# Re-ordering and re-placing a Strassen transformer block: score tiles key half first, and PSUM banks as halves of two-bank tiles

## The chip, the cores and the metric

The kernel runs on one core of a Trainium2 chip. The metric is the time of one execution on the device in microseconds (us); three executions of the kernel before took 662.69, 663.8 and 662.54 us, a median of 662.69. A core has five engines that run at the same time, each its own instruction queue in order: TensorE (PE) multiplies matrices into PSUM, which has eight banks of 512 fp32 values on each of 128 partitions; VectorE (DVE), ScalarE (ACT) and GpSimd (POOL) do element-wise work, of which DVE and ACT read PSUM in this kernel and POOL works on SBUF alone; SyncE (SP) issues the DMAs. Engines wait for one another by semaphores, and an instruction that waits holds back all that stands behind it on its engine.

## What is computed

A cross-attention transformer block in fp32, for 8 sequences of 256 tokens with 512 features, and as many context tokens:

```python
x = layer_norm(hidden_states, ln1_w, ln1_b)
q = (x @ q_w + q_b)      # 16 heads of 32; k and v likewise from ctx
k = (ctx @ k_w + k_b)
v = (ctx @ v_w + v_b)
scores = einsum('bhqd,bhkd->bhqk', q, k) / sqrt(32)
attn = softmax(where(mask, scores, finfo.min))
hidden = einsum('bhqk,bhkd->bhqd', attn, v) @ cproj_w + cproj_b + hidden_states
y = layer_norm(hidden, ln2_w, ln2_b)
y = gelu_tanh(y @ fc_w + fc_b)          # 512 -> 2048
out = hidden + y @ proj_w + proj_b      # 2048 -> 512
```

## The kernel before

The 2048 tokens are done in two groups of 1024 (four sequences each), named by a digit g that is 0 or 1. Every large product goes by Strassen's scheme: a 2 x 2 block product is seven block products P1 to P7 of sums and differences of the blocks. The helper `quad` (L848) accumulates the seven in three PSUM banks X, Y, W and takes them out in steps that DVE or ACT do: `t1, c11, t2, t3, c22, c12, c21`. fc and proj use the scheme on two levels, so they have outer products 1 to 7 with inner products 1 to 7 each. The helper `sums` (L827) makes the sums of blocks; each such sum may be done by DVE (one instruction of 1024, 512 or 256 columns) or by POOL (where 1024 columns take two instructions of 512, L625 to L628).

Names in this document are built so: letters for the tile, then group and block. `c`, `x` and `y` are the transposed context, first-norm and second-norm tokens; `c0t`, `x1t`, `a0t` their block sums; `y0i1_2` the second inner sum of the first outer operand of fc in group 0; `fw` and `pw` the weights of fc and proj, `fw0i..`, `pw1i..` their sums, which go to DRAM and come back as `fl` and `pl` when wanted; `h` the hidden tiles of fc; `z` the sums of h for proj (`z1i4_4` is one); `fc011_P6`, `pd14_P4`, `q1_0_P6` and `v0_0_P1` are products of fc, proj, q and v; `turn_y0_10` is a group of PE transposes through PSUM.

Attention runs in 32 units, each four heads of one sequence. In a unit, `scores` (L1009) and `attend` (L1057) issue:

- `s`: 16 row-tiled matmuls give scores with keys on partitions, in four banks (one per head), each with two key halves of 256 queries.
- `ev`: eight ACT instructions take these out with the mask bias into two SBUF tiles `pr` of 1024 columns, two heads each.
- `mx`, `mt`, `mc`, `fold`: DVE and ACT reduce to the maximum over the keys. It is stored (`md`) and loaded back broadcast to all partitions (`mm`, four heads of 256 queries).
- `less`: subtracts the maximum, for each `pr` by one DVE instruction of 1024 (L1042) or two POOL instructions of 512 (L1047).
- `exp`: one ACT instruction of 1024 per `pr` (L1050).
- `av`: 32 column-tiled matmuls, half of them giving the row sums with a block of ones; `r` (three DVE instructions, L1073 to L1076) inverts the sums and `att` (DVE) scales.

The order of all work is written out by hand. `PROGRAM` (L124) lists 2953 operations; each engine's queue is the subsequence of its operations, and a suffix `:A`, `:V` or `:G` chooses ACT, DVE or POOL where there is a choice. `PLACES` (L355) gives every buffer its SBUF slot or PSUM bank. `Order.run` (L94) reads both, and the program is issued in that order. A buffer in a place waits for the last readers of the buffer that had the place before. SBUF slots of kind "Q" have 1024 columns, and buffers of kind "P" (512) are halves of such a slot's tile (`halves`, in `tile_of`, L556). PSUM had two kinds, three banks "W" for `quad` and five "C" for the rest, though `PLACES` may name a bank of the other kind for a buffer; each buffer is a new [128, 512] tile of its bank.

The main loops, from the end of the kernel's body: inputs and attention of group 0, q, k, v of group 1, sums of fc's weights, attention of group 1, output projection and second norm of group 0, fc of group 0, sums of proj's weights, the same for group 1, proj of group 0, fc and proj of group 1. `PROGRAM` interleaves these streams. Attention of group 1 (units 1..) thus overlaps `y0` and the first fc products.

Of the kernel before, what the change touches and what calls it, by code (L numbers as in the profile page):

```python
# [10 lines left out]
F32 = mybir.dt.float32  # L11
# [5 lines left out]
P = 128  # L17
# [6 lines left out]
BANKS = {"W": 3, "C": 5}  # L24
# [19 lines left out]
class Order:  # L44
# [49 lines left out]
    def run(self):  # L94
# [30 lines left out]
cq0_00_1 cq0_00_0 vw00 cq0_01_1 cq0_01_0 rows8 rows7 cq0_10_0 turn_c0_00 rows0 turn_c0_10 c0_00:A cq0_10_1 c0_10:V  # L125
cq0_11_0 small v0_0_P1 cq0_11_1 kw01 turn_c0_11 fw0_01_0 v0_1_P1 c0_11:A vw11 rows5 turn_c0_01 rows2 turn_c0_30
vw10 c0_01:A turn_c0_20 mk c0_30:A c0t1:G c0_20:V v0_0_t1:A vw01 turn_c0_21 v0_1_t1:V turn_c0_31 fw0_11_1 k0_0_P2
c0_21:V rows3 c0_31:V c0t2:V kw10 k0_1_P2 rows4 kw11 c0t3:V kw00 rows6 v0_0_P2 vws1:V fw0_10_0 c0t4:V fw0_00_0
v0_1_P2 vws2:V fw0_00_1 kws1:V xt0_3 rows1 k0_1_P1 fw0_10_1 kws2:V mk~1 xt0_0 kws3:V fw0_11_0 v0_0_c11 fw0i1_1:G
v0_1_P6 fw1_00_1 vws4:V xt0_2 fw0i1_2:V fw0s3:V fw1_00_0 k0_0_P1 v0_1_t2:A xt0_6 fw0i7_1:V fw1_10_0 v0_1_c11  # L130
fw0i7_2:G fw1_11_0 cols v0_1_P5 cols~1 qw10 k0_0_t1:V qw11 fw0i7_4:V fw0s1:V xt0_1 v0_0_P6 v0_1_t3:A fw1_11_1
fw0s2:V fw1_10_1 xt0_5 k0_0_P6 fw0i6_3:V xt0_4 k0_1_t1:V fw0i6_1:G cb fw0i5_1:G v0_1_P3 k0_0_t2:V kws4:G fw0i1_4:V
k0_1_P6 stats_x0_30 fw0i1_3:G fw1i1_1:V stats_x0_00 fw0i6_2:G k0_0_P5 fw1i1_3:V k0_1_t2:A xt0_7 v0_0_t2:V fw1i1_2:G
fw0_01_1 stats_x0_10 fw1i1_4:G fcd0_1_True aggr_x0_30 k0_1_P5 fw1i4_1:V qw01 aggr_x0_00 stats_x0_01 fw1i4_2:G
fw1_01_0 fw0i6_4:V fcd0_6_False stats_x0_11 k0_1_P7 k0_1_t3:A fw1_01_1 aggr_x0_01 fw0i7_3:V k0_0_t3:A eps_x0_0
fcd0_7_False stats_x0_31 pow_x0_0 qw00 aggr_x0_31 k0_1_P3 fw1i4_4:G k0_1_c22 fcd0_7_True fw0i5_2:G aggr_x0_11
fcd0_5_False nb_x0_0 k0_0_c11 fw0i5_4:G norm_x0_01:A v0_0_P5 aggr_x0_10 k0_1_c11 fw0i2_1:G norm_x0_00:A fw1i4_3:V
k0_1_c12:A fw0i2_2:V k0_0_P7 eps_x0_1 eps_x0_3 fw0i5_3:V stats_x0_20 pow_x0_3 stats_x0_21 pow_x0_1 k0_0_P3 nb_x0_3
nb_x0_1 fw0i2_3:V norm_x0_31:A aggr_x0_20 aggr_x0_21 eps_x0_2 fw0i2_4:V norm_x0_10:A pow_x0_2 k0_0_c22 fcd0_2_True
k0_1_P4 v0_0_t3:V fw1i2_1:G fcd1_4_True k0_0_c12:A fcd0_6_True norm_x0_11:A nb_x0_2 fw0s4:V kd0_0_11 k0_0_P4  # L140
fcd1_1_True vws3:V norm_x0_20:A fcd0_3_False fw1i2_2:V fcd0_5_True norm_x0_21:A qws1:V turn_x0_10 norm_x0_30:A
fw1i2_4:G k0_0_c21 turn_x0_00 x0_10:A turn_x0_20 turn_x0_30 x0_20:A v0_0_P3 x0_30:V qws3:G xt1_2 cb1_02 x0_00:V
v0_1_c12:A fw0i3_1:V turn_x0_31 fw1i2_3:V turn_x0_11 fw0i3_2:V x0_31:A turn_x0_21 fw1s1:V turn_x0_01 q0_0_P1
x0_01:A qws2:G v0_0_c12:V fcd1_5_False x0_21:A k0_1_c21 fcd1_2_True fw1i5_3:G cb1_20 x0_11:A q0_0_P2 cb1_03
q0_0_t1:A x0t1:V q0_1_P1 fw0i3_3:V q0_0_c11 x0t2:V s000 fw0i3_4:V x0t3:V q0_0_P6 ev000_11 ev000_31 fw1s3:V xt1_3
ev000_10 ev000_01 cb1_12 q0_0_P7 x0t4:V kd0_0_21 q0_0_t2:A fcd1_7_False q0_1_t1:A fw1s2:V ev000_21 ev000_00 q0_0_P5
mx000_0 fw1s4:G fcd1_6_False cb1_10 q0_1_P6 q0_0_t3:A ev000_30 q0_0_c22 ev000_20 stats_x1_10 fcd1_3_False q0_1_P2
fw1i3_3:V fw1i5_1:V q0_1_t2:V fw1i5_2:G mx000_1 q0_0_P4 fw1i6_1:G qws4:G q0_1_c11 q0_1_P5 q0_0_c21 fw1i5_4:V mt000
fw0i4_3:G fcd1_5_True mc000_3 mc000_2 s020 cb1_13 mc000_1 fw1i6_3:G fold000 cb1_00 fw1i7_1:V q0_0_P3 md000 ev020_30
fw0i4_1:V ev020_21 fw1i7_2:V cb1_23 ev020_00 fw0i4_2:G cb1_21 ev020_10 fw1i7_4:G ev020_20 cb1_01 q0_1_P7 ev020_01  # L150
cb1_11 fw1i3_1:G ev020_31 q0_0_c12:A mx020_1 fw1i6_2:G ev020_11 s002 fw1i3_2:G mm000 mx020_0 fw0i4_4:G v0_1_P7
fw1i7_3:G mt020 stats_x1_11 mc020_2 mc020_3 fw1i6_4:G q0_1_t3:V ev002_30 ev002_11 fw1i3_4:G aggr_x1_10 aggr_x1_11
v0_0_P7 mc020_1 q0_1_c22 ev002_01 ev002_00 fold020 ev002_10 eps_x1_1 md020 ev002_31 pow_x1_1 ev002_20 q0_1_P3
fcd1_7_True v0_0_c22 ev002_21 cb1_31 nb_x1_1 mx002_0 less000_1:G mm020 s022 mx002_1 cb1_33 cb1_22 v0_0_P4 ev022_20
cT1_10 cb1_32 ev022_30 cT1_00 ev022_11 cb1_30 less000_0:G ev022_31 mt002 v0_1_c22 ev022_21 q0_1_P4 ev022_00 mx022_1
mc002_2 ev022_01 ev022_10 less020_0:G mx022_0 v0_1_P4 mt022 q0_1_c21 mc022_2 mc022_3 s010 mc022_1 v0_0_c21 mc002_3
# [24 lines left out]
ev023_30 mc003_1 ev023_10 att012 ev023_11 xT1_20 s011 exp001_0 fold003 mx023_0 md003 v1_1_P2 ev011_00 mm021
ev011_31 xb1_12 ev011_11 ev011_20 xb1_11 exp001_1 v1_1_P3 xb1_03 v1_1_c11 ev011_30 mx023_1 ev011_01 ev011_21
# [329 lines left out]
def tile_xattn_block(  # L512
# [986 lines left out]
```

## Time and profile before

| | |
|---|---|
| three runs | 662.54, 662.69, 663.8 us |
| profiled execution, span from first to last instruction | 662.0 us |
| mean granted clock of TensorE | 1.000 |
| busy PE / DVE / POOL / ACT | 654.6 / 585.7 / 374.8 / 342.4 us |
| DMA | 144.84 MB, mean 219 GB/s, 206586 packets |
| median landing time of a broadcast maximum (`mm`, 512 KB) | 5.1 us |
| median landing time of a proj weight block (`pl`, 256 KB) | 4.2 us |

The profile is of one execution of its own, for which only the span is given. The difference between a run's time and the span lies ahead of the first and behind the last instruction of the trace. Engine busy times overlap, so they don't add up to the span. In group rows, "out<-in" are tile names without their numbers, then shapes, count, total busy us, mean ns of one, and idle time ahead of them with what ended it.

### The profile page before, as it was taken

What the parts mean: (1) busy time and instruction counts of PE and PEld (TensorE: products, weight loads), DVE (VectorE), ACT (ScalarE), POOL (GpSimd) and SP (SyncE); (2) the same over time, 40 slices, a digit from 0 to 9 for tenths busy, and PEclk for the clock granted to TensorE, in tenths of its full rate; (3) what the DMA queues carried; (4) which work ended last, traced back from release to release, by engine and by line L of the source; (5) the groups of instructions that cost most, each with busy time, mean ns of one, the idle gap of its engine ahead of it and who ended that gap; (6) DMA issues with size and microseconds to landing.
All of it is one profiled execution on the core that took longest, in us unless ns stands there. A gap on an engine that the chain in (4) does not pass through costs nothing.

```text
span 662.0 us, 11469 instructions
## 1 busy us (share of the span) xinstructions
PE 654.6 (99%) x3925; PEld 490.0 (74%) x3925; DVE 585.7 (88%) x980; ACT 342.4 (52%) x702; POOL 374.8 (57%) x340
## 2 busy tenths in 40 slices
PE   8999999999999999999999999999999999999997
PEld 7746554477544776777688888888888888888887
DVE  2998799999999999999999998997789787998775
ACT  2046479799999899866995572030020013930000
POOL 1262773646888997699958774423535217720260
PEclk9999999999999999999999999999999999999999
DMA  8999888786574467886878698889978779359366
GB/s 250 311 356 307 211 197 291 267 255 125 144 241 161 144 202 234 263 268 197 266 249 273 198 235 225 289 269 230 195 193 241 190 201 242 93 142 240 106 141 111
DMA packets 206586, 144.84 MB, mean 219 GB/s; under 512 B 117008, under 2 KB 166976, under 8 KB 206528
## 3 DMA queue, kind: packets, MB, share of 16 engines
q1 hardware_dynamic: 206528, 144.11, 76.8%
q8 instruction: 31, 0.51, 0.3%
q14 instruction: 27, 0.22, 0.1%
HBM read 104.10 MB, written 39.98 MB: 218 GB/s over the span
## 4 chain that ended last, share of the span: by engine, by line
PE 92%; DVE 5%; ACT 1%; DMA 1%; issue 0%; SPq 0%; POOL 0%; DVEq 0%; ACTq 0%
PE pd_X L639 15%; PE fc_X L639 14%; PE fc_W L639 8%; PE av L639 7%; PE pd_W L639 7%; PE s L639 4%; PE o_X L639 4%; PE q_X L639 4%; PE k_X L639 4%; PE v_X L639 4%; PE pd_Y L639 4%; PE fc_Y L639 4%; PE q_W L639 2%; PE k_W L639 2%; PE v_W L639 2%; PE o_W L639 2%
## 5 line engine op out<-in xcount | busy, mean ns | idle before, releaser
L1047 POOL TENSOR_TENSOR pr<-pr,mm 128x512 f32<-128x512 f32 x84 | 110.4, 1346 | 22.8 <-DMA mm<-md 9.2
L619 ACT ACTIVATE pr<-s,cols 128x256 f32<-128x256 f32 x256 | 104.5, 482 | 21.8 <-PE s L639 15.8
L1022 DVE TRANSPOSE_TENSOR_REDUCE mx<-pr 128x32 f32<-128x1024 f32 x64 | 77.6, 1223 | 3.3 <-ACT pr L619 3.3
L1227 ACT ACTIVATE h<-h,cols 128x256 f32<-128x256 f32 x128 | 54.1, 498 | 36.7 <-DVE h L630 36.6
L1050 ACT ACTIVATE pr<-pr 128x1024 f32<-128x1024 f32 x64 | 66.9, 1069 | 3.4 <-POOL pr L1047 2.8
L630 DVE TENSOR_TENSOR h<-fc_X,h 128x512 f32<-128x512 f32 x80 | 52.8, 679 | 6.2 <-PE fc_X L639 5.5
L630 DVE TENSOR_TENSOR h<-fc_W,h 128x512 f32<-128x512 f32 x48 | 32.0, 679 | 5.8 <-PE fc_W L639 5.3
L639 PE MATMUL av<-pr,ones 128*32 128x256 f32 x512 | 34.2, 384 | 0.7 <-ACT pr L1050 0.6
L1029 ACT COPY mx<-mx 32x64 f32<-32x64 f32 x96 | 23.1, 243 | 19.8 <-DVE mx L1026 15.8
L1042 DVE TENSOR_TENSOR pr<-pr,mm 128x1024 f32<-128x1024 f32 x22 | 30.8, 1407 | 0.0
L628 POOL TENSOR_TENSOR z1i<-h,z1i 128x512 f32<-128x512 f32 x4 | 5.7, 1440 | 40.4 <-PE pd_X L639 40.4
L639 PEld LDWEIGHTS av<-pr,ones 128*32 128x32 f32 x512 | 14.1, 109 | 18.5 <-issue 6.7
L630 POOL TENSOR_TENSOR h<-h,fl 128x512 f32<-128x512 f32 x9 | 11.5, 1295 | 24.6 <-DVE fl L630 15.0
L639 PE MATMUL fc_W<-y1i,fl 128*128 128x256 f32 x100 | 24.6, 380 | 0.0
L639 PE MATMUL fc_X<-y1i,fl 128*128 128x256 f32 x88 | 21.6, 381 | 0.0
L639 PEld LDWEIGHTS fc_W<-y1i,fl 128*128 128x128 f32 x100 | 18.9, 190 | 2.9 <-DVE h L630 0.3
L639 PE MATMUL pd_W<-z0i,pl 128*128 128x256 f32 x88 | 20.6, 379 | 0.0
L1030 DVE TENSOR_REDUCE mx<-mx 32x32 f32<-32x256 f32 x32 | 18.4, 574 | 1.4 <-ACT mx L1029 1.3
L639 PE MATMUL pd_X<-z0i,pl 128*128 128x256 f32 x80 | 18.9, 379 | 0.0
L606 ACT COPY fl<-fc_X 128x512 f32<-128x512 f32 x6 | 3.5, 580 | 29.5 <-PE fc_X L639 29.2
L639 PEld LDWEIGHTS fc_X<-y1i,fl 128*128 128x128 f32 x88 | 16.6, 190 | 2.6 <-ACT h L606 0.2
L639 PEld LDWEIGHTS pd_W<-z0i,pl 128*128 128x128 f32 x88 | 16.7, 190 | 2.3
(595 smaller groups left out, 1815.6 us busy)
## 6 DMA issues: line engine op xcount, KB each, us to landing
mm<-md SPq DMA_DIRECT2D x32, 512.0 KB, 5.1
pl<-prd SPq DMA_DIRECT2D x47, 256.0 KB, 4.2
fl<-fcd SPq DMA_DIRECT2D x41, 256.0 KB, 4.0
fl<-prd SPq DMA_DIRECT2D x24, 256.0 KB, 3.8
fw<-in_L_xattn_fc_w_dram SPq DMA_DIRECT2D x16, 256.0 KB, 4.9
pw<-in_L_xattn_proj_w_dram SPq DMA_DIRECT2D x32, 128.0 KB, 3.6
hid<-in_x_dram SPq DMA_DIRECT2D x8, 512.0 KB, 4.8
hd<-hid SPq DMA_DIRECT2D x8, 512.0 KB, 3.4
```

The costliest lines, as they stand in the source:

```text
L606: (nc.scalar.copy if e == "ACT" else nc.vector.tensor_copy)(to(), of_())
L619: lambda e: nc.scalar.activation(to(), of_(), AF.Identity, bias=bias(), scale=1.0))
L628: nc.gpsimd.tensor_tensor(to()[:, ts(k, 512)], in0()[:, ts(k, 512)], in1()[:, ts(k, 512)], op)
L630: E[e].tensor_tensor(to(), in0(), in1(), op)
L639: nc.tensor.matmul(o(), l(), r(), start=first, stop=True, skip_group_check=True)
L1022: T.op(f"mx{u}_{h}", [("DVE", 1.126)], [(pr[h], None)], [(mx, [h])], lambda e, h=h: nc.vector.tensor_reduce(tile_of(mx)[:, 0:64].rearrange ...
L1029: lambda e, a=a: nc.scalar.copy(tile_of(mx)[0:32, 64 + 64 * a : 128 + 64 * a], tile_of(mx)[32 * a : 32 * a + 32, 64:128]))
L1030: T.op(f"fold{u}", [("DVE", 0.38)], [(mx, [2, 3, 4, 5])], [(mx, [6])], lambda e: nc.vector.tensor_reduce(tile_of(mx)[0:32, 320:352], tile_ ...
L1042: nc.vector.tensor_tensor(p_, p_, m_[:, :, None, :].to_broadcast([P, 2, 2, S]), ALU.subtract)
L1047: E[e].tensor_tensor(p_, p_, at(M, j)[:, None, :].to_broadcast([P, 2, S]), ALU.subtract)
L1050: lambda e, h=h: nc.scalar.activation(tile_of(pr[h]), tile_of(pr[h]), AF.Exp), table="exp")
L1227: lambda e, f=f, b=b, c=c: nc.scalar.activation(at(h[f][b], c), at(h[f][b], c), AF.Gelu_apprx_tanh, bias=col(c_fcb + f * 4 + c), scale=1.0 ...
```

## The change

Four things change, all in one file.

1. PSUM's eight banks become four tiles of two banks each ([128, 1024], tags B0 to B3), and a buffer of kind "W" or "C" is one half of such a tile, in any of the eight. A kind "D", a whole pair, is defined; no buffer uses it. The target of the warm-up matmuls is the first pair.
2. In a `pr` tile the key half becomes the outer index: block 2 * kc + j instead of 2 * j + kc (j is the head in the tile). Evictions, maximum, `less` and `av` follow. `less` on POOL takes one key half of two heads per instruction instead of one head's two key halves.
3. `PROGRAM` is written anew. The 2953 operations are the same by name; their order differs everywhere, and 221 of them change engine. By engine: ACT 692 to 685, DVE 913 to 896, POOL 250 to 274 operations. By kind (DVE before to after, POOL before to after): `less` 22 to 18, 42 to 46; y sums (256) 16 to 10, 40 to 46; pw sums (256) 18 to 13, 38 to 43; z inner sums (1024) 42 to 39, 14 to 17; z block sums (1024) 26 to 24, 6 to 8; a sums (1024) 3 to 6, 5 to 2; c sums (1024) 5 to 3, 3 to 5; qws 1 to 4, 3 to 0; kws 3 to 1, 1 to 3; vws 4 to 2, 0 to 2. Among the operations that go from DVE to POOL are x1t3, y0i1_2 and y0i7_2. The warm matmuls `small`, behind `turn_c0_10` before, stand first. Exp and gelu alternate less often on ACT.
4. `PLACES` is written anew: all slots and banks.

```diff
-BANKS = {"W": 3, "C": 5}
+BANKS = ("W", "C", "D")
...
-                    w = where[b.name]
-                    b.home = w[0] if not w[0].isdigit() else b.kind
-                    b.slot = int(w.lstrip("WC"))
+                    b.slot = int(where[b.name])
...
 PROGRAM = """
-cq0_00_1 cq0_00_0 vw00 cq0_01_1 cq0_01_0 rows8 rows7 cq0_10_0 turn_c0_00 rows0 turn_c0_10 c0_00:A cq0_10_1 c0_10:V
-cq0_11_0 small v0_0_P1 cq0_11_1 kw01 turn_c0_11 fw0_01_0 v0_1_P1 c0_11:A vw11 rows5 turn_c0_01 rows2 turn_c0_30
+small cq0_00_0 cq0_00_1 vw00 rows0 turn_c0_00 c0_00:A cq0_01_0 turn_c0_10 cq0_01_1 c0_10:A v0_1_P1 cq0_11_0 turn_c0_01
+c0_01:V rows6 turn_c0_11 rows4 cq0_11_1 kw00 cq0_10_0 mk v0_0_P1 rows2 turn_c0_31 c0_11:V c0t1:G mk~1 turn_c0_21
...
     T = Order()
     E = {"PE": nc.tensor, "DVE": nc.vector, "ACT": nc.scalar, "POOL": nc.gpsimd, "SP": nc.sync}
 
-    halves = {}
+    halves, twos = {}, {}
 
     def tile_of(b):
         if b.t is None:
                 b.t = halves[s][:, ts(k, 512)]
             elif b.kind in SLOTS:
                 b.t = slots.tile([P, SLOTS[b.kind][1]], F32, tag=f"{b.kind}{b.slot}", name=b.name)
+            elif b.kind == "D":
+                b.t = banks.tile([P, 1024], F32, tag=f"B{b.slot // 2}", name=b.name)
+                twos[b.slot // 2] = None
             else:
-                b.t = banks.tile([P, 512], F32, tag=f"{b.home}{b.slot}", name=b.name)
+                s, k = divmod(b.slot, 2)
+                if twos.get(s) is None:
+                    twos[s] = banks.tile([P, 1024], F32, tag=f"B{s}", name=b.name)
+                b.t = twos[s][:, ts(k, 512)]
         return b.t
 
     def at(b, i, n=1, w=256):
     make_identity(nc, ident.t)
     warm = const.tile([P, 64], F32, name="warm")
     nc.vector.memset(warm, 1.0)
-    first = banks.tile([P, 512], F32, tag="W0", name="first")
+    twos[0] = banks.tile([P, 1024], F32, tag="B0", name="first")
+    first = twos[0]
 
     def small(n):
         for _ in range(n):
         pr = [Buf(f"pr{u}_{h}", "Q", 4) for h in range(2)]
         for kc in range(2):
             for j in range(4):
-                copy(f"ev{u}_{j}{kc}", (pr[j // 2], [2 * (j % 2) + kc]), (sb[j], [kc]), lambda j=j, kc=kc: at(pr[j // 2], 2 * (j % 2) + kc),
+                copy(f"ev{u}_{j}{kc}", (pr[j // 2], [2 * kc + j % 2]), (sb[j], [kc]), lambda j=j, kc=kc: at(pr[j // 2], 2 * kc + j % 2),
                      lambda j=j, kc=kc: at(sb[j], kc), 256, lambda kc=kc: col(2 * (4 * g + b) + kc))
         mx = Buf(f"mx{u}", "mx", 7)
         for h in range(2):
             T.op(f"mx{u}_{h}", [("DVE", 1.126)], [(pr[h], None)], [(mx, [h])], lambda e, h=h: nc.vector.tensor_reduce(
-                tile_of(mx)[:, 0:64].rearrange("p (k j q) -> p j k q", k=2, j=4)[:, 2 * h : 2 * h + 2],
+                tile_of(mx)[:, 0:64].rearrange("p (k j q) -> p k j q", k=2, j=4)[:, :, 2 * h : 2 * h + 2],
                 tile_of(pr[h]).rearrange("p (n r) -> p n r", r=32), axis=mybir.AxisListType.X,
                 op=ALU.max, apply_transpose=True))
         T.op(f"mt{u}", [("DVE", 0.15)], [(mx, [0, 1])], [(mx, [2])], lambda e: nc.vector.transpose(tile_of(mx)[:, 64:128], tile_of(mx)[:, 0:64]))
         ss = Buf(f"ss{u}", "Q", 2) if halves else None
         for h in range(2):
             def less(e, h=h):
+                m_ = at(M, 2 * h, 2)
                 if e == "DVE":
-                    p_ = tile_of(pr[h]).rearrange("p (i k q) -> p i k q", i=2, k=2)
-                    m_ = tile_of(M)[:, 512 * h : 512 * h + 512].rearrange("p (i q) -> p i q", i=2)
-                    nc.vector.tensor_tensor(p_, p_, m_[:, :, None, :].to_broadcast([P, 2, 2, S]), ALU.subtract)
+                    p_ = tile_of(pr[h]).rearrange("p (k n) -> p k n", k=2)
+                    nc.vector.tensor_tensor(p_, p_, m_[:, None, :].to_broadcast([P, 2, 512]), ALU.subtract)
                     return
-                for i in range(2):
-                    j = 2 * h + i
-                    p_ = at(pr[h], i, 1, 512).rearrange("p (k q) -> p k q", k=2)
-                    E[e].tensor_tensor(p_, p_, at(M, j)[:, None, :].to_broadcast([P, 2, S]), ALU.subtract)
+                for k in range(2):
+                    p_ = at(pr[h], k, 1, 512)
+                    E[e].tensor_tensor(p_, p_, m_, ALU.subtract)
             T.op(f"less{u}_{h}", [("POOL", 2.448), ("DVE", 1.16)], [(pr[h], None), (M, None)], [(pr[h], None)], less, lock=True, pieces=2)
             T.op(f"exp{u}_{h}", [("ACT", 0.947)], [(pr[h], None)], [(pr[h], None)],
                  lambda e, h=h: nc.scalar.activation(tile_of(pr[h]), tile_of(pr[h]), AF.Exp), table="exp")
             if halves:
-                two = lambda h=h: tile_of(pr[h]).rearrange("p (i k q) -> p i k q", i=2, k=2)
+                two = lambda h=h: tile_of(pr[h]).rearrange("p (k i q) -> p k i q", i=2, k=2)
                 plus(f"ss{u}_{h}", (ss, [h]), (pr[h], None), (pr[h], None), lambda h=h: at(ss, h, 1, 512).rearrange("p (i q) -> p i q", i=2),
-                     lambda two=two: two()[:, :, 0, :], lambda two=two: two()[:, :, 1, :], 512, pool_too=True)
+                     lambda two=two: two()[:, 0], lambda two=two: two()[:, 1], 512, pool_too=True)
         return u, v, pr, ss
 
     def attend(g, hg, b, u, v, pt, ss):
             sums_ = [(lambda j=j: tile_of(av)[j * HD : (j + 1) * HD, 256:512], lambda: ones, lambda j=j: at(ss, j), True) for j in range(4)]
         else:
             sums_ = [(lambda j=j: tile_of(av)[j * HD : (j + 1) * HD, 256:512], lambda: ones,
-                      lambda j=j, kc=kc: at(pt[j // 2], 2 * (j % 2) + kc), kc == 0) for kc in range(2) for j in range(4)]
+                      lambda j=j, kc=kc: at(pt[j // 2], 2 * kc + j % 2), kc == 0) for kc in range(2) for j in range(4)]
         mm(f"av{u}", 1.36 if ss else 1.72, [(v[0], None)] + ([(ss, None)] if ss else []) + [(p_, None) for p_ in pt], [(av, None)], sums_ + [
             (lambda j=j: tile_of(av)[j * HD : (j + 1) * HD, :256], lambda j=j, kc=kc: v[1]()[:, kc, j * HD : (j + 1) * HD],
-             lambda j=j, kc=kc: at(pt[j // 2], 2 * (j % 2) + kc), kc == 0)
+             lambda j=j, kc=kc: at(pt[j // 2], 2 * kc + j % 2), kc == 0)
             for kc in range(2) for j in range(4)], mode="col")
         R = Buf(f"r{u}", "H")
         rc = Buf(f"rc{u}", "sm")
```

More of the change, by code (lines that the diff above doesn't have):

```diff
@@ L127 @@
[L127 to L156, printed above, removed]
@@ new lines @@
+x1_30:A x1_20:A q1_0_P6 vu013 ev033_00 mt013 mc013_3 r003 x1t3:G hid0_3 q1_1_t1:A exp011_0 vu011 mc013_2 att003
+ev033_30 q1_0_P2 mc013_1 q1_0_t2:V md031 exp011_1 fold013 hid0_2 q1_1_P6 q1_0_c11 mm031 q1_0_P5 xb0_2:V less023_1:G
+md013 mx033_1 exp023_1 ev033_10 q1_0_t3:A s100 ev100_11 ev100_21 ev100_20 mx033_0 q1_0_P3 pw0_00_00 mt033 ev100_30
+r021 less023_0:G ev100_01 att021 ev100_10 ev100_31 q1_0_P7 q1_0_c22 q1_1_t2:A exp023_0 x1t4:G mc033_1 less031_1:G
+ev100_00 q1_0_c12:A ab0_100 mx100_1 av011 mx100_0 exp031_1 mc033_2 r011 ow11 av023 mt100 mc033_3 fold033 mc100_1
@@ new lines @@
+norm_y0_21:A y0_30:A fc001_P1 fc011_P1 hd1 fc001_P2 r102 y0_20:A fc001_t1:A av112 less132_1:V fc011_t1:A mx101_1
+prd0_7_False r110 norm_y0_31:A norm_y0_30:A y0i1_1:G y0i1_2:G fc011_P2 fc011_c11 att102 att110 fc011_P6 mt101
+norm_y0_20:A pw0i2_1:G pw0i7_1:G pw0i2_2:G exp132_1 pw0i7_3:G pw0i2_4:G fc001_c11 exp132_0 mc101_1 pw0i7_2:G mc101_2
+mc101_3 fc001_P6 r112 fold101 s121 av132 fc011_t2:A att112 fl016_0 y0i1_4:G ev121_30 fc001_t2:A fl016_2 ev121_11
+ev121_31 turn_y0_11 turn_y0_31 ev121_10 fc001_P5 fl012_0 y0_11:A ev121_21 pw0s1:V pw0i2_3:V ev121_01 pw0s2:V fc011_P5
@@ new lines @@
+fc005_P4 fc007_P1 pw1_00_11 pw1i1_1:G gelu0_100 mx113_1 gelu0_002 pw1_00_00 pw1i1_3:G ev133_00 y0i7_2:G ev133_01
+mx113_0 fc015_c21 prd1_4_True fc005_P3 ev133_31 mt113 fc005_c21 ev133_11 fc017_P1 pw1_00_01 fc007_t1:A mc113_2
+pw1i1_2:V pw1s2:V pw1_01_01 mc113_1 ev133_10 fc017_t1:A fc007_P6 fc017_P6 pw1i1_4:G mc113_3 fold113 mm131 fc007_t2:A
+fc007_P2 md113 fc017_t2:A fc017_P5 fc017_t3:A fc007_P5 pw1s3:V fl017_1 pw1i2_3:G fc007_t3:A less131_1:V fc007_c11
+pw1i2_1:G prd1_1_True less131_0:V y0i3_1:G fc017_P2 exp131_1 fc007_11~1:G fc017_c11 y0i7_4:V fl003_0 fc007_P3
@@ L462 @@
[L462 to L465 removed]
+cq0_00=84 cq0_10=26 cq0_01=78 cq0_11=52 ps_cols=7 ps_c0_00=5 c0_00=6 ps_c0_10=6 ps_c0_20=6 c0_10=42 ps_c0_30=7
@@ new lines @@
+av033=1 r033=5 rc033=5 cb1_0=56 c1_00=52 c1_01=54 cb1_1=30 cb1_2=22 c1_10=56 c1_11=74 cb1_3=88 xt1_0=44 xt1_1=17
+xt1_2=61 xt1_3=65 xt1_4=61 xt1_5=45 xt1_6=46 xt1_7=63 st_x1_0=7 mv_x1_0=2 rs_x1_0=3 xn_x1_00=51 xn_x1_01=40 st_x1_1=9
+mv_x1_1=0 rs_x1_1=9 xn_x1_10=11 xn_x1_11=26 st_x1_2=1 mv_x1_2=0 rs_x1_2=7 xn_x1_20=5 xn_x1_21=19 st_x1_3=6 mv_x1_3=1
+rs_x1_3=6 xn_x1_30=15 xn_x1_31=10 xb1_0=2 x1_00=66 x1_01=4 xb1_1=18 xb1_2=58 x1_10=68 x1_11=2 xb1_3=14 c1t1=30 c1t2=8
+c1t3=26 c1t4=80 x1t1=56 x1t2=84 x1t3=66 x1t4=44 k1_0_X=1 k1_0_11=86 k1_0_Y=0 k1_0_21=65 k1_0_W=3 k1_0_22=35 k1_0_12=0
@@ L466 @@
+ps_o10=2
 """
```

613 lines of the change are left out of this document (307 added, 306 removed).

## The prediction

> **What bounds the kernel now.** I read the page's first part and its chain first, to see which engine sets the end.
>
> ```profile
> span 662.0 us, 11469 instructions
> PE 654.6 (99%) x3925; PEld 490.0 (74%) x3925; DVE 585.7 (88%) x980; ACT 342.4 (52%) x702; POOL 374.8 (57%) x340
> PE 92%; DVE 5%; ACT 1%; DMA 1%; issue 0%; SPq 0%; POOL 0%; DVEq 0%; ACTq 0%
> ```
>
> TensorE (PE) is busy for 654.6 of 662.0 us. The change adds no matmul and removes none, so all that an order of work can win is PE's idle time, 662.0 - 654.6 = 7.4 us, and all that it can lose is new idle time. The next view, busy time by stretches of 20 us (columns: stretch, its length, then busy time of PE, PEld, DVE, ACT, POOL), says where the 7.4 us lie.
>
> ```profile
> 0.00:20.00 20.00, 18.28 (x105) 14.79 (x106) 7.70 (x11) 4.02 (x6) 3.31 (x10) 1.00 0.82 252
> ...
> 240.00:260.00 20.00, 18.95 (x236) 12.95 (x232) 19.42 (x49) 19.26 (x37) 17.48 (x17) 1.00 0.75 234
> 260.00:280.00 20.00, 19.51 (x164) 14.12 (x157) 19.49 (x35) 17.39 (x34) 14.11 (x15) 1.00 0.80 265
> 280.00:300.00 20.00, 19.38 (x133) 15.04 (x132) 19.65 (x32) 13.18 (x30) 18.62 (x21) 1.00 0.74 241
> ...
> 640.00:662.00 22.00, 18.64 (x98) 16.42 (x96) 14.24 (x32) 0.00 (x0) 0.00 (x0) 0.99 0.62 119
> ```
>
> The head lacks 20 - 18.28 = 1.72 us, the tail 22 - 18.64 = 3.36, the stretch 240 to 300 lacks 1.05 + 0.49 + 0.62 = 2.16. That is 7.24 of 7.4. In the middle stretch, where the attention of the second group overlaps the second layer norm and the first fc products of the first group, DVE is busy 19.4 to 19.7 of 20 us and ACT up to 19.26: there PE waits because others are full. The granted clock is 1.00 in these rows, so a pace that changes with the clock plays no part in this kernel. PE's own waits (waiter, what it waited for: us in total, times, longest) name the places.
>
> ```profile
> PE ps_y L726 <- DVE att L630: 1.2, 2, 1.0
> PE first L651 <- DVE warm L646: 1.0, 1, 1.0
> PE av L639 <- ACT pr L1050: 0.6, 1, 0.6
> PE v_X L639 <- DMA vw<-in_L_xattn_v_w_dram: 0.5, 1, 0.5
> ```
>
> The first and third lie in the middle stretch, where PE's timeline (start, length, what, idle before and releaser) has them.
>
> ```profile
> 256.43 0.33 PE L726 MATMUL ps_y<-ident,xt 128*128 128x128 f32 x1
> ...
> 258.12 0.33 PE L726 MATMUL ps_y<-ident,xt 128*128 128x128 f32 x1 [1.00 <-DVE att L630]
> ...
> 282.00 1.34 PE L639 MATMUL s<-xn_x 32*128 32x256 f32 x16
> 283.96 1.07 PE L639 MATMUL av<-pr,ones 128*32 128x256 f32 x16 [0.62 <-ACT pr L1050]
> ```
>
> A transpose of y0 waits for its bank, which an `att` on DVE is the last to read, and av101 waits for the exp of its unit. The chain of waits just behind, in order of time (start, us, what), gives PE's real pace.
>
> ```profile
> 269.58 0.87 PE ps_y L726 x8
> 270.45 0.86 PE fc_X L639 x4
> 271.31 0.86 PE fc_W L639 x4
> 272.18 1.08 PE s L639 x16
> 273.25 1.86 PE av L639 x32
> 275.12 1.06 PE fc_W L639 x4
> ```
>
> Matmul ends are modelled, so I check the two waits by pace. Eight transposes take 0.87 us undisturbed; those begun at 256.43 should have reached their fifth at 256.43 + 4 x 0.109 = 256.87, and it began at 258.12: 1.25 us lost, where the view says 1.0. A score unit takes 1.08 us, so av101 could have begun at 282.00 + 1.08 = 283.08 and began at 283.96: 0.88 lost, where the view says 0.6. By pace losses are some 1.3 times the view's. The 2.16 us of this stretch are then worth 2.2 to 2.9 us, and I put 4 as the most.
>
> **The change part by part.** Base: the span, 662.0. The three runs have a median of 662.69 (662.54 to 663.8), 0.7 above the span; I work on the span and add 0.7 at the end.
>
> *The head.* The four warm matmuls (eight pieces) named `small` move from behind the second transposes to the very front.
>
> ```profile
> 2.75 1.49 PE L651 MATMUL first<-warm 128*64 128x64 f32 x12
> 4.44 1.93 PE L726 MATMUL ps_c<-ident,cq 128*128 128x128 f32 x8 [0.20 <-DMA cq<-in_ctx_dram]
> 6.30 0.68 PE L651 MATMUL first<-warm 128*64 128x64 f32 x8
> 7.51 1.75 PE L639 MATMUL v_X<-vw,c 128*128 128x256 f32 x7 [0.53 <-DMA vw<-in_L_xattn_v_w_dram]
> ```
>
> They look like 0.68 us to be saved, but the first v product behind them waits 0.53 us more for a weight block, whose load is third in SP's queue in both orders. What hides the saving is that DMA. At the front the pieces end at about 4.24 + 0.68 = 4.92 instead of 4.24 and the transposes begin up to 0.48 us later, still done by 4.92 + 1.93 = 6.85, ahead of 7.51. I take 0, between -0.5 and +0.5 (the same block's load a little earlier or later).
>
> *The table of layouts.* A unit's score tiles are laid out with the key half outermost, so subtracting the maximum reads contiguous 512-wide rows of it instead of a 256-wide row twice. Counts and sizes of instructions stay. The rows say that the broadcast form cost nothing:
>
> ```profile
> L1042 DVE TENSOR_TENSOR pr<-pr,mm x22: 1169/1217/2324, 105.3 to 377.2; 128x1024 f32<-128x1024 f32 x22
> L1047 POOL TENSOR_TENSOR pr<-pr,mm x84: 1258/1278/2767, 85.1 to 318.2; 128x512 f32<-128x512 f32 x84
> L630 DVE TENSOR_TENSOR z1i<-z1t,z1t x8: 1214/1217/1539, 584.2 to 648.0; 128x1024 f32<-128x1024 f32 x8
> L628 POOL TENSOR_TENSOR z1i<-z1t,z1i x2: 1267/1270/1273, 636.7 to 638.0; 128x512 f32<-128x512 f32 x2
> ```
>
> The medians (min/median/max, ns) are 1217 against 1217 of a plain add on DVE, 1278 against 1270 on POOL. The maximum, evictions and `av` only use other column offsets. Together 0; at most 22 x 0.05 us on DVE, which is under the bounds below.
>
> *The banks.* The eight PSUM banks become halves of four two-bank tiles, and any buffer may take any bank. No instruction writes or reads a whole pair. The cost is 0 if dependencies go on being kept by region, as they are for the 512-wide SBUF buffers, which already are halves of shared tiles. If they went by tile it would be large; that is a rival.
>
> *Who does what.* 221 operations change engine. Net, DVE gives up four of 22 `less`, eleven 256-wide sums (six y, five pw) and five 1024-wide z sums, and takes three a sums, four pd evictions and small change: -4 x 1.22 - 11 x 0.41 - 5 x 1.22 = -15.5 us, and -13 with the rest. POOL takes the same things at its own price, in pairs of 512: +4 x 2.56 + 11 x 0.73 + 5 x 2.54 = +31, and +36 with the rest. The 256-wide prices are these:
>
> ```profile
> L630 DVE TENSOR_TENSOR pw1i<-pw1s x3: 410/411/649, 362.4 to 392.1; 128x256 f32<-128x256 f32 x3
> L630 POOL TENSOR_TENSOR pw1i<-pw x4: 721/728/734, 313.8 to 342.6; 128x256 f32<-128x256 f32 x4
> ```
>
> That is 36 of 375 us on an engine that idles 43% of the time, and 13 less on one that is full where PE waits. It helps only if the 13 come out of the stretch that waits. I added up the median interval of each operation that stands between PE's 240th and 285th us of work in the old and in the new list. DVE: 47.2 us of work in both (a `less` and two fc evictions more; a maximum, a sum and some statistics fewer). POOL: 38.5 before, 35.4 after. ACT: 37.0 in both. Over PE's 160th to 285th us DVE goes from 124.8 to 119.5 (two `less`, two maxima, three pw sums and two evictions fewer are most of it), POOL from 104.3 to 106.5. A maximum is this row:
>
> ```profile
> L1022 DVE TRANSPOSE_TENSOR_REDUCE mx<-pr 128x32 f32<-128x1024 f32 x64 | 77.6, 1223 | 3.3 <-ACT pr L619 3.3
> ```
>
>  So DVE comes to the stretch less late, but is as full in it. Against that, setting each queue's running sum beside PE's, DVE falls at most 2.1 us behind in the old list and 3.2 in the new, both near PE's 270th to 285th us. The two readings disagree in sign; I take +0.5 for the stretch, with -4 (all its waits go) and +2 (the lag of 3.2 less 2.1, and as much again by collisions) as ends.
>
> In this trace DVE's `less` reaches 2324 ns from a floor of 1169, and POOL's 2767 from 1258: each slows the other. [...]
>
> *Switches of PE's mode.* An fc product behind an attention unit takes 1.06 us, behind another product 0.86 (rows at 275.12 and 271.31). The new list has one fewer such switch, 39 instead of 40: -0.2, at most -0.4.
>
> *Table loads.*
>
> ```profile
> L1227 ACT ACT_TABLE_LOAD x5 | 6.4, 1283 | 0.1
> L1050 ACT ACT_TABLE_LOAD x4 | 5.1, 1283 | 0.1
> ```
>
> The order alternates less often between exp and gelu: 10 loads become 8, 2.6 us less on ACT. They lie where exp and gelu mix, behind some 290 us; PE's stretches are full there, and ACT is busy 13.2 of 20 us already in the stretch at 280. I take 0, with -0.9 as the end, the pace loss of the one exp that was late.
>
> *Queues.* SP issues the same loads and stores in another order. The new list names some POOL and SP operations up to 10 us behind the point where their inputs are ready, so that a waiting POOL operation holds back those queued behind it; this is the slower rival. The tail (last product, one eviction, three stores) stays: 0.
>
> Sum: 662.0 + 0 + 0 + 0 + 0.5 - 0.2 + 0 = 662.3, and with 0.7 663.0 us.
>
> **The rivals.** *Faster: the middle stretch is relieved.* DVE and POOL arrive at 240 us with 5.3 - 2.2 = 3 us less work between them, and a bank may come from any of eight, where the transpose at 258.1 waited for one. For it: those two waits name exactly DVE and a bank. Against it: 47.2 us of DVE work in 45 us either way. It gives 662.0 - 0.2 - 2.9 + 0.7 = 659.6, at most (4) 658.5.
>
> *Slower: POOL becomes late where PE needs it.* This trace has these rows for the sums of the second group's normalized tokens (the last says who waited for them):
>
> ```profile
> L630 DVE TENSOR_TENSOR x1t<-x,x x1: 2110/2110/2110, 175.8 to 175.8; 128x1024 f32<-128x1024 f32 x1
> L628 POOL TENSOR_TENSOR x1t<-x,x1t x4: 1266/1368/2266, 175.3 to 190.1; 128x512 f32<-128x512 f32 x4
> ...
>   PEld q_X L639: 0.3, 1
> ```
>
> In the new list x1t3 goes to POOL behind x1t2, which itself stands behind a `less` that waits for the broadcast of its maximum, and q1_0_P6 needs x1t2. y0i1_2 (for fc011_P6) and y0i7_2 (for fc007_P6) go from DVE to POOL, behind `less` pairs and a sum that waits for a load. By list I find those three 0 to 2 us late, and z1i4_4, POOL's last sum ahead of pd14_P4, some 2 us early. The mechanism decides where a `less` pair or sum pair (2.5 us, up to 4.5 by the 2266) stands between inputs and a product with less slack than that. One such place costs 1.3 us (a pair less DVE's time), two or three 2.6 to 4; against it stands that these sums delay PE's weight loads by only 0.3 us today. It gives 663.0 + 3 = 666.0, up to 667.5.
>
> *Slower by much: dependencies by whole tile.* The price is this row's:
>
> ```profile
> L630 DVE TENSOR_TENSOR h<-fc_X,h 128x512 f32<-128x512 f32 x80 | 52.8, 679 | 6.2 <-PE fc_X L639 5.5
> L630 DVE TENSOR_TENSOR h<-fc_W,h 128x512 f32<-128x512 f32 x48 | 32.0, 679 | 5.8 <-PE fc_W L639 5.3
> ```
>
> If a product had to wait for evictions out of the neighbouring bank, each would cost up to the 0.68 us of an h eviction; for a third of the 128 evictions of fc alone 0.68 x 43 = 29 us, so over 690. Against it stand the SBUF halves.
>
> **How the numbers follow.** About 0.2%, 1.3 us, is what a measurement of this kernel can tell from no change. No change (likeliest, 663.0, its own range 661.4 to 664.0): 0.36. Relief of the middle stretch (659.6): 0.33. POOL late (666.0): 0.27. Dependencies by tile: 0.04. So faster 0.33, same 0.36, slower 0.31. The range has to reach to both neighbours: low 658.7, near the end of relief, and high 667.0, near the end of POOL late, leaving out the tile case and the tips.
>
> **What would show it.** Right: PE's busy time within 1 us of 654.6, the head's first v product at 7.5, idle of 1.5 to 3.5 us between 240 and 300, still released by DVE or ACT; `less` medians within 3% of 1217 and 1278; eight table loads. POOL's busy time up by 30 to 40 us without POOL among PE's releasers. Wrong on the slow side: PE or PEld waiting for POOL at q1_0_P6, fc011_P6, fc007_P6 or pd14_P4. Wrong on the fast side: no wait for DVE in the y0 transposes and under 1 us idle from 240 to 300. Wrong altogether: PE's span without waits changes, by a pace of matmuls other than 0.86 us for four, or many short waits for evictions everywhere.

## The result, and the profile after

The changed kernel takes 828.0 us (median of 4 runs, 821.36 to 829.84) against 663.25 (662.54 to 663.96, a fourth run added to the three above): a ratio of 1.2456, 95% interval 1.24 to 1.2513. It is slower by 165 us where I forecast no change and put 4 in 100 on the mechanism that did it. The profiled execution is the quickest of the four, 821.36 us, with a span of 819.6. Its page:

```profile
span 819.6 us, 11436 instructions
PE 698.8 (85%) x3925; PEld 499.4 (61%) x3925; DVE 588.3 (72%) x963; ACT 342.6 (42%) x693; POOL 420.2 (51%) x373
PE 64%; DVE 18%; ACT 9%; issue 4%; DMA 3%; SPq 1%; POOL 1%; DVEq 0%; ACTq 0%; POOLq 0%
```

TensorE does the same 3925 matmuls and idles 120.8 us instead of 7.4. Its busy time rose as well, from 654.6 to 698.8 us: part of that is matmuls at a lower clock (at 0.50, eight took 3.78 us where eight before them took 1.89; last section), the rest wasn't separated. Of the chain that ends last it holds 64% instead of 92%, and DVE and ACT share 27%. No engine is full any more: DVE fell from 88% to 72%. That is the sign of engines that wait for each other. The stretches (columns as before; the last three are the granted clock, the DMA engines' busy share and GB/s) show that it happens everywhere, not only in the stretch at 240 us:

```profile
140.00:180.00 40.00, 31.64 (x204) 18.18 (x203) 25.77 (x49) 19.97 (x40) 17.91 (x15) 0.87 0.61 151
180.00:220.00 40.00, 31.61 (x202) 21.06 (x202) 25.97 (x43) 27.05 (x60) 18.20 (x14) 0.87 0.36 78
440.00:480.00 40.00, 30.92 (x172) 22.91 (x172) 24.41 (x39) 16.07 (x26) 19.22 (x22) 0.96 0.44 140
760.00:800.00 40.00, 37.74 (x171) 32.09 (x172) 24.50 (x43) 0.00 (x0) 19.09 (x16) 1.00 0.64 138
```

TensorE's waits, five of many rows. The names are no longer of use for the bank: all buffers of a pair carry the name of the tile's first user, since they are halves of it. `first` is one pair, and `ps_c` stands for all three others.

```profile
PE ps_c L636 <- ACT pr L616: 21.6, 19, 3.5
PE ps_c L636 <- DVE h L627: 14.1, 16, 3.9
PE first L636 <- DVE h L627: 7.4, 9, 2.0
PE ps_c L636 <- DVE att L627: 7.3, 3, 4.5
PE first L636 <- ACT pr L616: 7.0, 6, 4.1
```

`ACT pr L616` is the eviction of scores. In the trace of before no matmul is listed as idle for one. Two engines that only read PSUM wait for each other too:

```profile
DVE rc L1070 <- ACT pr L616: 14.1, 7, 3.8
```

The row sums of an `av` bank have nothing to do with an eviction of scores, which lies in another bank. One place in full, from the timelines of TensorE and ACT:

```profile
160.73 1.98 PE L636 MATMUL ps_c<-c1t,kw 128*128 128x512 f32 x4
162.56 1.89 PE L636 MATMUL ps_c<-vw,c 128*128 128x256 f32 x8
168.59 3.78 PE L636 MATMUL first<-v,c1t 128*128 128x256 f32 x8 [4.14 <-ACT pr L616]
172.16 3.01 PE L636 MATMUL ps_c<-v,c1t 128*128 128x256 f32 x8
```

```profile
164.40 0.47 ACT L616 ACTIVATE pr<-ps_c,cols 128x256 f32<-128x256 f32 x1 [0.76 <-DVE xt L603]
...
168.06 0.47 ACT L616 ACTIVATE pr<-first,cols 128x256 f32<-128x256 f32 x1
```

A score unit had put one head into a bank of the pair `first`. A v product that goes to the pair's other bank waits 4.14 us until ACT has read the last score out of it (168.06 + 0.47 = 168.53; it starts at 168.59). The eviction at 164.40 had itself waited for DVE to copy a product out of the other bank of its own pair.

The compiled program says how often this is asked for. I took each wait of TensorE on ACT or DVE and looked at the instruction that raises the semaphore to the awaited value: in 181 cases it touches only the other bank of the pair (164 touch the same bank, and the rest are data in SBUF, always in an overlapping region). ACT and DVE have 140 such waits on TensorE, and 100 on one another.

### The profile page after: what moved, and what is told of

Its sections match the earlier page's. It is cut to its first block, busy times and chain, and to the rows that moved or that the text cites. A ratio compares the mean times of both kernels' runs of the same rounds, so it can differ in the third digit from the quotient of the medians.

```text
span 819.6 us, 11436 instructions
## 1 busy us (share of the span) xinstructions
PE 698.8 (85%) x3925; PEld 499.4 (61%) x3925; DVE 588.3 (72%) x963; ACT 342.6 (42%) x693; POOL 420.2 (51%) x373
## 4 chain that ended last, share of the span: by engine, by line
PE 64%; DVE 18%; ACT 9%; issue 4%; DMA 3%; SPq 1%; POOL 1%; DVEq 0%; ACTq 0%; POOLq 0%
PE ps_c L636 46%; PE first L636 17%; ACT pr L616 5%; DVE h L627 4%; DVE mx L1020 2%; ACT pr L1047 1%; DVE rc L1070 1%; DVE z0i L627 1%; SPq L590 1%; DVE r L1073 1%; ACT mx L1027 1%; PE ps_c L724 1%; DVE z1i L627 1%; DVE po L627 1%; DVE att L627 1%
## 5 line engine op out<-in xcount | busy, mean ns | idle before, releaser
L616 ACT ACTIVATE pr<-ps_c,cols 128x256 f32<-128x256 f32 x212 | 90.6, 477 | 71.4 <-PE ps_c L636 46.6
L627 DVE TENSOR_TENSOR h<-ps_c,h 128x512 f32<-128x512 f32 x113 | 75.3, 682 | 39.1 <-PE ps_c L636 36.9
L627 DVE TENSOR_TENSOR po<-ps_c,po 128x256 f32<-128x256 f32 x49 | 19.8, 415 | 23.3 <-PE ps_c L636 21.1
L636 PE MATMUL ps_c<-pr,ones 128*32 128x256 f32 x416 | 29.0, 396 | 6.7 <-ACT pr L616 4.8
L627 DVE TENSOR_TENSOR h<-first,h 128x512 f32<-128x512 f32 x39 | 26.3, 680 | 11.5 <-PE first L636 9.9
L636 PE MATMUL ps_c<-z0i,pl 128*128 128x256 f32 x128 | 29.6, 379 | 0.0
L636 PE MATMUL ps_c<-z1i,pl 128*128 128x256 f32 x104 | 24.7, 383 | 3.2 <-DVE po L627 1.7
L616 ACT ACTIVATE pr<-first,cols 128x256 f32<-128x256 f32 x44 | 20.6, 477 | 15.9 <-PE first L636 9.1
L636 PEld LDWEIGHTS ps_c<-z0i,pl 128*128 128x128 f32 x128 | 24.3, 190 | 3.3
L636 PE MATMUL ps_c<-y1i,fl 128*128 128x256 f32 x92 | 23.8, 389 | 1.3 <-DVE h L627 1.3
```

The lines of the kernel that those rows point to most:

```text
L616: lambda e: nc.scalar.activation(to(), of_(), AF.Identity, bias=bias(), scale=1.0))
L627: E[e].tensor_tensor(to(), in0(), in1(), op)
L636: nc.tensor.matmul(o(), l(), r(), start=first, stop=True, skip_group_check=True)
```

## The experiments

My theory T: an access to a two-bank PSUM tile is made to wait for accesses to either bank of it. Rivals: O, the new order and places cost the time; H, physically neighbouring banks disturb each other on the chip. Ratios are to the kernel before, run on the same chip.

**New one-bank tiles** under the changed order, places and layout:

```diff
-                s, k = divmod(b.slot, 2)
-                if twos.get(s) is None:
-                    twos[s] = banks.tile([P, 1024], F32, tag=f"B{s}", name=b.name)
-                b.t = twos[s][:, ts(k, 512)]
+                b.t = banks.tile([P, 512], F32, tag=f"B{b.slot}", name=b.name)
...
```

> The changed kernel with its order, places and layout, but each buffer a new one-bank tile (eight tags B0 to B7, banks as in its places) instead of half of a two-bank tile. Theory T (the two-bank tiles make an access to one bank wait for accesses to the other bank of its pair): the whole loss of 165 us goes; what is left is the effect of order, places and layout, which I forecast as 663.0, so 658.7 to 667.0. Rival O (the new order or places cost the time, by late sums on GpSimd or by buffers that wait for each other): stays above 800. Rival H (physically neighbouring banks disturb each other on the chip): the banks lie as before the edit, so it stays above 800 as well.

666.07 us, ratio 1.0016 (0.9983 to 1.0049). The whole loss goes with the tiles, and O falls; H stays open, since the buffers did not keep their physical banks. The waits come back to a handful (its page and TensorE's waits):

```profile
span 662.7 us, 11453 instructions
PE 650.4 (98%) x3925; PEld 490.8 (74%) x3925; DVE 578.2 (87%) x963; ACT 337.4 (51%) x693; POOL 418.1 (63%) x373
```

```profile
PE ps_y L720 <- ACT xn_y L812: 1.4, 2, 1.0
PE v_X L633 <- DMA vw<-in_L_xattn_v_w_dram: 1.3, 1, 1.3
...
PE fc_X L633 <- POOL y0i L624: 0.2, 1, 0.2
```

**Two-bank tiles alone**, in the kernel before (W0 to W2, C0 to C4 as halves 0 to 7).

> The kernel before, its order, places and layout untouched, with only the two-bank tiles put in (W0 to W2 and C0 to C4 become halves 0 to 7 of four pairs). T: slower by as much as its own pairs couple. Its program has 144 waits of TensorE on ACT or DVE whose awaited instruction touches only the other bank of the pair, against 181 in the changed kernel, so 165 x 144 / 181 = 131 us: about 795, between 740 and 850. O: 663, since the order is the old one. H: 663, if banks lie as before.

737.14 us, ratio 1.1084 (1.102 to 1.1149): 72 us, the sign right, the size little more than half of the 131 expected, and the time just below the range. T holds; what sets its price was open. TensorE's waits for evictions are fewer and shorter here; the two costliest rows:

```profile
PE ps_c L642 <- ACT pr L622: 9.5, 10, 1.6
PE v_X L642 <- ACT pr L622: 5.8, 7, 1.5
```

**The layout alone**, in the kernel before.

> The kernel before with only the layout of the score tiles changed (key half outermost, in evictions, maximum, subtraction and av). T and O both: no change, 662 to 664, medians of the subtraction on DVE within 1217 +- 30 ns and on GpSimd within 1278 +- 30 ns. A rival, that reading a contiguous row of the maximum is quicker, gives 0.03 to 0.1 us for each of 22 on DVE and 84 on GpSimd: 655 to 661 if half of that lies on the path.

666.25 us, ratio 1.0019 (0.9987 to 1.0051): above the 662 to 664 expected, but the kernel before took 664.81 on that chip, so no change that can be told. The rows of POOL and DVE in this run:

```profile
L1046 POOL TENSOR_TENSOR pr<-pr,mm x84: 1257/1274/2762, 85.4 to 321.0; 128x512 f32<-128x512 f32 x84
```

```profile
L1042 DVE TENSOR_TENSOR pr<-pr,mm x22: 1170/1214/2305, 105.6 to 379.9; 128x1024 f32<-128x1024 f32 x22
```

The medians are 1274 and 1214 ns where they were 1278 and 1217.

**Two tiles of four banks** in the changed kernel (`divmod(b.slot, 4)`, 2048 columns).

> The changed kernel with two tiles of four banks each instead of four of two. T: each access now waits for three other banks; waits on instructions in other banks go from 181 to some 260 (TensorE on ACT or DVE) and the time goes up again, to between 950 and 1200. O and H: as the changed kernel, 815 to 840, since order and physical banks stay.

1065.66 us, ratio 1.6005 (1.5885 to 1.6124). The dose goes the way of T.

**Kept one-bank tiles** in the changed kernel, partners side by side (`twos[k] = banks.tile([P, 512], ...)` for k from 0 to 7 at the start, then `b.t = twos[b.slot]`).

> The changed kernel with eight one-bank tiles, made once at the start in the order 0 to 7 and kept for the whole program, as the two-bank tiles are. Contrary to what I wrote for the run with new one-bank tiles, that run's buffers did not lie in the changed kernel's physical banks (its banks 0 to 7 held places 0, 5, 6, 1, 3, 4, 7, 2); here they do, so only the width of the tile differs from the changed kernel. T (width of the tile): 661 to 668, as with new one-bank tiles. H (physical neighbours disturb each other): above 800. K (a tile that is kept instead of made anew keeps too many dependencies): above 700.

666.55 us, ratio 1.0017 (0.9989 to 1.0045). Same order, the same partners in neighbouring banks, tiles kept for the whole program: H and K fall. The expectation is wrong in that these are the changed kernel's own physical banks: in the compiled programs banks 0 to 7 hold the places 0, 1, 4, 5, 6, 7, 2, 3 in the changed kernel and 0 to 7 here, so that three of the pairs lie elsewhere, each still together. In this program no wait of TensorE on ACT or DVE is for an instruction that touches only another bank, where the changed kernel has 181. The width of the tile is the cause.

**The tail on two queues.** In the run with one-bank tiles the last block product ended early and the span did not. The run stands beside one more of that kernel (664.33 us, a single execution):

> The run with new one-bank tiles once more, as the neighbour of the next one on the same chip: 663 to 668.

```diff
-            name, [("SP", 0.47)], src, [(d, keys)] if d else [],
-            lambda e: nc.sync.dma_start(to(), of_()), serve=served(name, mb), base=1.4,
+            name, [("SP", 0.47), ("ACT", 0.47)], src, [(d, keys)] if d else [],
+            lambda e: (nc.scalar if e == "ACT" else nc.sync).dma_start(to(), of_()), serve=served(name, mb), base=1.4,
...
```

> New one-bank tiles, and every second of the sixteen late output stores (so1) issued by ACT, which is idle there, instead of SyncE. In the run with one-bank tiles TensorE's last product ends at 655.9 us, 2.7 us earlier than in the kernel before (658.6), but the span ends at 662.7, because SyncE issues stores without a pause from 649 us and reaches the last one only at 658.2, 1.9 us after its data. If the queue of SyncE holds the end (Q): 2 to 3.5 us less than with one-bank tiles, a ratio of 0.995 to 0.998 to the kernel before. If the landing of the stores holds it (L, DMA engines are 0.8 to 0.9 busy there): no change, ratio 1.000 to 1.003.

665.55 us, ratio 1.0021 (0.999 to 1.0051): no gain, as L had it. Its queues issue side by side and take as long:

```profile
646.58 9.88 ACTq L593 DMA_DIRECT2D out_dram<-tq  x8
647.81 9.56 SPq L593 DMA_DIRECT2D out_dram<-tq  x7
```

Eight issues take 9.9 us on one queue and seven 9.6 on the other, where one queue had issued thirteen in 10.7. From 653 to 664 us the DMA engines are 0.7 to 0.9 busy in all slices of 0.65 us but one. That fits transfers that set the pace; by what limit wasn't tried.

**One pair only** (places 0 and 1) and six one-bank tiles.

> The changed kernel with one two-bank tile (places 0 and 1) and six one-bank tiles. T, if the waits of the pairs add up: its program has 49 waits of TensorE on an access to the other bank, against 181, so 165 x 49 / 181 = 45 us, about 709 (690 to 730). T, if one pair's waits are mostly hidden in the slack of the other banks: 670 to 690. O: above 800.

704.41 us, ratio 1.0575 (1.0495 to 1.0655): 39 us for 49 waits, 0.8 us each, near the 0.9 of the changed kernel (165 / 181). The price of pairs adds up.

**Other partners.** Is the number of waits the price?

> The changed kernel, its order and places, with other partners in the two-bank tiles: places 0 and 4, 1 and 3, 2 and 7, 5 and 6 share a tile. Of the 105 ways to pair eight banks this one gives the fewest waits of TensorE on an access to the partner bank, 142; the changed kernel's own has the most, 181. N (the number of such waits prices it, 0.78 to 0.91 us each as with one pair and with four): 663 + 142 x 0.78 to 0.91 = 774 to 792. P (which buffers meet, not how many, prices it): the time lies clear of that, anywhere from 730 to 850.

817.93 us, ratio 1.2271 (1.2175 to 1.2368): 152 us for 142 waits, 1.07 each. N fails: fewer waits, hardly less time.

> The kernel before with two-bank tiles, with the partners that give the most waits of TensorE on the partner bank, 172 instead of 144. N: 0.5 us each as with its first pairing (72 us for 144), so 663 + 86 = 749 (740 to 760). If the price for each is that of the changed kernel, 0.78 to 0.91: 797 to 820; then it is the pairing, and not the order of work, that made the first pairing cheap.

749.91 us, ratio 1.1251 (1.1127 to 1.1375): 84 us for 172 waits, 0.49 each, as with the first pairing of the old order (72 / 144 = 0.5). So a wait costs 0.5 us in the old order and about twice that in the new one, whoever the partners are. That pointed to the common list: from it the waits are made, and only in the old kernel does it stand nearly in order of time.

**The list sorted by time**, every engine's sequence untouched.

> The changed kernel with its two-bank tiles, every engine's own sequence of operations untouched, but the common list written in the order in which the operations started in the run with one-bank tiles. In the kernel before the list stands nearly in that order (for TensorE, ACT and DVE an operation stands behind one that starts later by 0.05 us on the mean, 1.5 at most); in the changed kernel it does not (0.63 on the mean, 28 at most). Theory S (an access waits for every earlier one in the list to the partner bank, so an operation listed far ahead of its time holds the partner's later ones back): the 175 waits now cost what they cost in the kernel before, 0.5 us each: 663 + 88 = 751 (735 to 770). Rival W (what a wait costs is set by the engines' own sequences and by the partners): stays at 815 to 835.

750.5 us, ratio 1.127 (1.1228 to 1.1312): 85 us for 175 waits, 0.49 each. S holds, W falls. The longest of TensorE's waits for evictions halve (1.7 and 2.0 us, from 3.5 and 3.9):

```profile
PE ps_c L635 <- ACT pr L615: 12.1, 14, 1.7
PE ps_c L635 <- DVE h L626: 7.4, 9, 2.0
```

> Control: the same re-written list with new one-bank tiles. The engines' sequences are those of the earlier runs with one-bank tiles and no wait between banks exists, so S and W both expect no change: 663 to 668.

666.09 us, ratio 1.0012 (0.9991 to 1.0032): without shared tiles the place in the list, with the same sequences, costs nothing.

So the 165 us are two things. About 85 are false waits between banks of a pair, which lists in or near order of time pay too (72 to 85 in three runs). About 80 come from how the list is written. That the order of the list is the cause is shown by the two sorted runs; how it acts is S, argued: a wait is for every access that stands earlier in the list, so an operation that stands ahead of its time (28 us at most) holds back later accesses to the partner bank. TensorE's longest listed wait is 5.1 us. A part of the 80, at most some 13 by the estimate of the last section, may be the clock. No version beat the kernel before; those with one-bank tiles are within its noise or some 1 us slower.

## Why the prediction was wrong

**The banks: wrong, and all of the loss.** The step read: "The cost is 0 if dependencies go on being kept by region, as they are for the 512-wide SBUF buffers, which already are halves of shared tiles." The condition was the whole question, and I answered it with a row of another memory. In the same compiled program every wait of TensorE on SBUF data is for an overlapping region, while 181 on PSUM are not. No trace of before could show it, for there no PSUM tile was wider than a bank. A cost that the trace cannot show should have been bounded from both sides and the range drawn through it; I gave it 4 in 100 and left it outside. The last of the prediction's signs of being wrong altogether, many short waits for evictions everywhere, is what came.

**The price of that rival: mis-sized.** I reckoned 43 evictions of fc at 0.68 us, 29 us, and "over 690". There are 181 waits on other banks, in all stages, and 165 / 181 = 0.9 us of loss for each; of the five rows of TensorE's waits above, evictions of scores have 25 waits and additions into h 25. The count was a quarter, because I priced one kind of buffer where every buffer shares a tile. That the unit price was near is luck: in a list in order of time it is 0.49, and the rest is the list's, for which the prediction had no term.

**Order, places and engines: the time right, in part by luck.** The forecast without pairs was 663.0 against 662.69, +0.3 us. Measured is a ratio of 1.0016 (0.9983 to 1.0049), +1.1 us, not to be told from none. By part, in the run with one-bank tiles:

```profile
0.00:20.00 20.00, 17.73 (x104) 13.73 (x105) 7.31 (x12) 5.09 (x8) 5.05 (x12) 1.00 0.81 242
...
240.00:260.00 20.00, 17.83 (x218) 11.84 (x217) 19.09 (x47) 18.67 (x33) 15.50 (x15) 1.00 0.57 178
260.00:280.00 20.00, 20.00 (x167) 14.97 (x166) 19.65 (x37) 18.84 (x37) 15.40 (x16) 1.00 0.84 283
280.00:300.00 20.00, 19.33 (x133) 15.01 (x132) 19.07 (x31) 11.69 (x30) 18.84 (x22) 1.00 0.86 281
...
640.00:662.70 22.70, 15.93 (x86) 14.02 (x84) 13.04 (x29) 0.00 (x0) 7.03 (x5) 0.93 0.57 104
```

- The head: the first v product waits 1.3 us for its load instead of 0.5, and starts at 7.09 us instead of 7.51; the warm matmuls saved show up as waiting, as said. The first 20 us lack 2.27 us instead of 1.72, a little more than the 0.5 allowed.
- The middle stretch lacks 2.17 + 0 + 0.67 = 2.84 us against 2.16: +0.7, forecast +0.5. The wait for `att` is gone, and one for the normalized rows (`xn_y`) has its place. The rival "relieved" fell.
- POOL's busy time rose by 43.3 us (36 forecast) and DVE's fell by 7.5 (13 forecast); what of the differences is mutual slowing wasn't measured (in the trace of before, a `less` of 2324 ns on DVE overlaps one of 2257 ns on POOL, where the medians are 1217 and 1278). POOL holds TensorE's matmuls up for 0.2 us in all: the rival "POOL late" fell.
- Seven table loads stand at gelu and exp (4 and 3) where nine stood before; with the one at the start that makes eight, as said. An effect on the time isn't seen.
- The tail, put at 0, grew: its stretch lacks 22.70 - 15.93 = 6.77 us instead of 3.36. TensorE was busy for 650.4 us, 4.2 less than before (650.4 to 653.9 in the five profiles with this order and one-bank tiles), where 654.6 within 1 us was a sign of being right, and its last product ended at 655.9 us instead of 658.6, but the output stores behind it did not end earlier. Less busy time and a longer tail, both put at nothing by the sum, nearly cancel, and that is luck. Why the busy time fell is open.

## What to carry to other kernels

In these programs a buffer that becomes a view of a wider PSUM tile inherits the waits of everything in that tile, readers against readers included (181 waits of TensorE for the other bank alone, and 100 of ACT and DVE on one another). Compare the waits in the compiled program before believing that dependencies go by region, and prove it for the memory in question. If wide PSUM tiles are wanted, keep the issue list in the order in which things happen: that alone was worth 78 us here (828.0 to 750.5). And an untested condition that touches every operation belongs inside the range, however unlikely it looks.

## What the runs showed of the hardware

The granted clock fell, which the prediction's sum had no term for: 0.975 on the mean in the profiled execution (0.962 to 0.967 in the other three), 0.87 from 140 to 220 us, 0.906 with four-bank tiles. After the pause of 4.14 us above, eight matmuls took 3.78 us where the eight before it took 1.89, half the pace, and the next eight still 3.01. The stretches around it (the third column from the end is the clock):

```profile
164.40:167.80 3.40, 0.04 (x1) 0.00 (x0) 3.37 (x5) 2.75 (x6) 0.50 (x1) 0.97 1.04 233
167.80:171.20 3.40, 2.61 (x6) 2.16 (x7) 1.85 (x2) 3.33 (x6) 3.40 (x3) 0.50 0.87 123
171.20:174.60 3.40, 3.40 (x10) 2.66 (x10) 2.14 (x3) 0.58 (x1) 2.03 (x2) 0.53 0.03 3
174.60:178.00 3.40, 3.40 (x55) 2.03 (x57) 2.16 (x4) 0.84 (x2) 0.00 (x0) 1.00 0.87 155
```

The clock is at half for some 6.8 us. It is at 0.97 in the first stretch, while TensorE pauses, and at 0.50 in the next, in which the pause of 4.14 us ends (at 168.59); it is back at 1.00 from 174.6 us, after some 6 us of matmuls (168.59 to 174.6).

Half pace is seen behind a shorter pause too. With two-bank tiles and the sorted list, four matmuls behind a pause of 1.99 us took 2.08 us, where the four before it took 1.03:

```profile
376.14 1.03 PE L635 MATMUL ps_c<-y0i,xn_x 128*128 128x256 f32 x4
379.16 2.08 PE L635 MATMUL ps_c<-y0i,fl 128*128 128x256 f32 x4 [1.99 <-DVE h L626]
```

With one pair or with two-bank tiles in the old order, 41 and 72 us longer in span, TensorE idled 40.8 and 58.1 us, its longest listed waits were 2.0 and 1.9 us, and the clock stayed at 0.999 and 0.998. With the fewest waits it idled 114.9 us at 0.966, in the changed kernel 120.8 us at 0.975. So the sum of the pauses alone doesn't give the clock in these profiles; what does is open.

As an estimate from these means, the clock is at most 0.025 x 819.6 = 20 us of the loss in the profiled execution; with the sorted list, at 0.990, it is at most 0.010 x 748.7 = 7 us, 13 less. It wasn't measured apart.
